# Seven-product blocks accumulated through three PSUM banks, and gram matrices on half columns, in a four-layer convolution/attention network

## The chip, the cores and the metric

The kernel runs on one core of a Trainium2 chip. A core has a matrix engine (TensorE, PE in the profile; its weight loads are listed apart as PEld), a vector engine (DVE), a scalar engine (ACT), a general engine (POOL) and a sync engine (SP) that issues transfers. Matrix products are written to PSUM, which here is eight banks of 128 partitions by 512 float32; DVE and ACT read PSUM, POOL does not in this kernel. All other tiles are in SBUF.

The metric is the device time of one execution in microseconds. The kernel before takes 1887.52 us, the median of three runs (1886.85 to 1887.64).

## What is computed

Eight images of 512 channels and 32 x 32 = 1024 positions, float32, go through four layers:

```python
# layer 0: f, g, h are 1x1 convolutions to 64 channels; batch norm and relu on f and g
z = einsum('bcn,bcm->bnm', f_x, g_x)
attn = z / svd(z)[:, 0]                       # divided by its largest singular value
z2 = einsum('bnm,bcm->bcn', attn, h_x)
x = conv1x1(z2, Wv, bv) + x
# layer 1: group norm, then attention over 1024 positions with 512 channels
h = group_norm(x); q, k, v = wq @ h, wk @ h, wv @ h
attn = softmax(q.T @ k * 512 ** -0.5); x = x + wp @ (v @ attn.T)
# layer 2: attention with 128 channels, then a projection and batch norm
t, p, g = split(W_w @ x); s = softmax(t.T @ p * 128 ** -0.5); x = x + bn(Z_w @ (g @ s.T))
# layer 3: products of signs, batch norm, residual, a PReLU
x = prelu(bn(sign(W) * mean|W| @ sign(x + bias)) + x)
```

## The kernel before

The program is traced in Python and unrolled whole. A planner in the framework orders the instructions of every engine by its own estimates of cost and inserts all waits between engines; the order of one engine in the trace is therefore not the order of the source, except for PE inside `with tc.manual_schedule(...)` (L1564), where it is written out by hand.

**The early part** (up to about 186 us). L1341 loads the eight images and forms f, g and h of each with 64-column products (`products`, L1351: two halves of an image on the two halves of the array's columns, out to partitions 0 to 63 and 64 to 127 of one bank). PSUM is split into 2 `wide` tiles of two banks and 4 single banks (L160). Images are handled in pairs j, two to a tile, 64 channels each. For each pair three gram matrices are made by `gram(j, i, lt, rhs)` (L1444): f with f (i = 0), g with g (i = 1), h with g (i = 2), each a sum over NT = 8 blocks of 128 positions. The largest singular value follows from powers of products of the first two: `first_chain(jl)` (L1128) for the pair that is used first, on full 128 x 128 matrices with zeros outside the two diagonal blocks; `chain(j)` (L1024) for the other three pairs, with its second operand as a 128 x 64 tile, its steps (`behind`) spread over the first batches.

The chain is a row of short dependent steps, so other work is set between its steps. `filler()` (L1534) is a generator of such pieces, called `todo`: two of transposes (`natural`), 16 of the weight product into `wu` (each one 128x128 by 128x512 product), the third gram of pair jl, a scaling (`scale_z`), the transposes and grams of the other pairs (`grams`, L1471, with sums of weights and biases beside them), and 16 pieces of the product into `wo`. `gram` yields twice, once after half of its blocks and once at its end, so that a gram is two pieces. Five pieces are taken before the first grams (L1555), 33 between the chain's 22 steps (L1568), and the last 25 in the first batch's entry (L1573).

The entry, `entering(0)` (L873), applies layer 0 to the first image and normalizes it: `weights0` (L293), four visits of `enter` (L409; each two products of 64 rows, L419, with a DVE addition L428 and statistics L431 for each), two tiny products for group means (L440, L447), then scale and shift (`rsqrt_eps`, L230), after which `normal` (L459) writes h, in pieces of 128x512 for the first batch, and the batches begin with `make_u` (L480). The other entries run inside the batch before.

**The batches** (eight times about 205 us). PSUM is eight single banks. Four products of each batch are written as a block scheme with seven block products in place of eight: `make_u` (2 of them), `scores1` (4), `make_v` (2) and the first part of `project2` (1), in all 9 a batch and 72 in the kernel. Each is a call of `seven` (L340). In it, `term(ps, ka, kb, first, last)` multiplies block ka of one operand with block kb of the other (2 products of 128x512, or 4 of 128x256 in `make_v`; two PE instructions for each) into a new bank if ps is None, or adds them onto what bank ps holds. In the order of the source, I number the terms 1 to 7:

1. A11 B11 into bank a; ACT copies it to c21 (L357)
2. S2 T2 into bank b; DVE adds c21 (L360)
3. S3 T3 into bank d; DVE adds c21, to c22 (L363)
4. S1 T1 into bank c; ACT copies it to c12 (L366), POOL adds c12 to c22 (L367)
5. A12 B21 onto bank a; ACT moves it to c11, or its exp (L371, L373)
6. S4 B22 onto bank c; DVE adds c21, to c12 (L376)
7. A22 T4 onto bank d; DVE adds c21 (L379)

The moves and sums are recorded at L346, L348 (`move`) and L352, L354 (`plus`), and all products at L395. So four banks are used, and three of them take a second product: bank a after three other terms, bank d after three, bank c after one (term 5). A product onto a bank waits for the read of it.

Between the terms stand other pieces: in `scores1` the last part of the batch before (`leave`) and the next batch's entry, of which each visit puts four additions and four statistics on DVE; in `make_u` almost everything of layer 2. `values1` (L547) follows `make_v`, with products in groups of four (L564).

Of the kernel before, what the change touches and what calls it, by code (L numbers as in the profile page):

```python
# [11 lines left out]
AF = mybir.ActivationFunctionType  # L12
ALU = mybir.AluOpType
# [3 lines left out]
P = 128  # L17
# [4 lines left out]
NT = N // P  # L22
# [3 lines left out]
MID = 64  # L26
# [59 lines left out]
def kernel(  # L86
# [17 lines left out]
    nc = tc.nc  # L104
    mm = nc.tensor.matmul
# [11 lines left out]
    def wide():  # L117
        return psum["wide"].tile([P, N], F32, tag="wide", name="wide")
# [4 lines left out]
    def bank():  # L123
        return psum["bank"].tile([P, HF], F32, tag="bank", name="bank")
# [17 lines left out]
    def half(i):  # L142
        return bass.ts(i, HF)

    def side(i):

        return slice(i * MID, (i + 1) * MID)
# [24 lines left out]
    def block_ones(size, value, name):  # L172

        n = P // size
        member = const.tile([P, n], F32, tag=name + "_m", name=name + "_m")
        nc.vector.tensor_reduce(
            member, ident.rearrange("p (g j) -> p g j", j=size), AX.X, ALU.add
        )
        t = const.tile([P, n, size], F32, tag=name, name=name)
        nc.vector.tensor_scalar(  # L180
            t, member.unsqueeze(2).to_broadcast([P, n, size]), value, None, ALU.mult
        )
        return t.rearrange("p g j -> p (g j)")

    mask2 = block_ones(MID, 1.0, "mask2")
# [44 lines left out]
    def rsqrt_eps(pool, var, n, name):  # L230
# [17 lines left out]
    gm = [keep.tile([P, P], F32, tag=f"gm{j}", name=f"gm{j}") for j in range(NPAIR)]  # L248
    gs_, gh_ = (
        [keep.tile([P, MID], F32, tag=f"{n}{j}", name=f"{n}{j}") for j in range(NPAIR)]  # L250
        for n in ("gg", "gh")
    )
    gg_full = keep.tile([P, P], F32, tag="gg_full", name="gg_full")
    sw3 = wpool.tile([P, CC, C // 2], F16, tag="sw3", name="sw3")
    round3 = const.tile([P, 1], F32, tag="round3", name="round3")
    nc.gpsimd.memset(round3, ROUND)
# [83 lines left out]
    def seven(term, c11, c12, c21, c22, b1=None, b2=None, exp=None, then=None):  # L340

        def move(dst, ps, bias):
            if bias is None:
                nc.scalar.copy(dst, ps)  # L346
            else:
                nc.scalar.activation(dst, ps, AF.Identity, bias=bias)  # L348

        def plus(ps, bias, u, dst):  # L350
            if bias is None:
                nc.vector.tensor_tensor(dst, ps, u, ALU.add)  # L352
            else:
                nc.vector.scalar_tensor_tensor(dst, ps, bias, u, ALU.add, ALU.add)  # L354

        pa, va = term(None, "A11", "B11", True, False)
        nc.scalar.copy(c21, va)  # L357
        yield
        _, vb = term(None, "S2", "T2", True, True)
        plus(vb, None, c21, c21)  # L360
        yield
        pd, vd = term(None, "S3", "T3", True, False)
        plus(vd, None, c21, c22)  # L363
        yield
        pc, vc = term(None, "S1", "T1", True, False)
        move(c12, vc, b2)  # L366
        nc.gpsimd.tensor_tensor(c22, c22, c12, ALU.add)  # L367
        yield
        term(pa, "A12", "B21", False, True)
        if exp is None:  # L370
            move(c11, va, b1)  # L371
        else:
            nc.scalar.activation(c11, va, AF.Exp, scale=exp)  # L373
        yield
        term(pc, "S4", "B22", False, True)
        plus(vc, b1, c21, c12)  # L376
        yield
        term(pd, "A22", "T4", False, True)
        plus(vd, b2, c21, c21)  # L379
        if then is not None:  # L380
            then()
        yield

    def product_of(lt, rhs, view=None, parts=1):

        def term(ps, ka, kb, first, last):
            fresh = ps is None
            if fresh:  # L390
                ps = bank()
            w = HF // parts
            for q in range(parts):
                for k in range(2):
                    mm(  # L395
                        out=ps[:, q * w : (q + 1) * w],
                        lhsT=lt(ka, kb, q, k),
                        rhs=rhs(ka, kb, q, k),
                        start=first and q == 0 and k == 0,
                        stop=last and k == 1,  # L400
                        skip_group_check=True,
                    )
            return ps, ps if view is None else view(ps)

        return term
# [117 lines left out]
    def scores1(env, hb, ua, es):  # L523

        scale = float(C) ** -0.5
        esum = env["small"].tile([P, N], F32, tag="esum", name="esum", bufs=1)
        for i in range(NTH):
            lo, hi = (env["e"].tile([P, N], F32, tag="e", name="e") for _ in range(2))
            es[i], es[NTH + i] = lo, hi
            term = product_of(  # L530
                lambda a, b, q, k: hb[b][:, k, bass.ts(i, P)],
                lambda a, b, q, k: ua[a][:, k, :],
            )

            yield from seven(
                term, lo[:, half(0)], hi[:, half(0)], lo[:, half(1)], hi[:, half(1)], exp=scale
            )
            nc.scalar.activation(lo[:, half(1)], lo[:, half(1)], AF.Exp, scale=scale)
            nc.scalar.activation(hi, hi, AF.Exp, scale=scale)
            if i == 0:  # L540
                nc.vector.tensor_tensor(esum, lo, hi, ALU.add)
            else:
                nc.vector.tensor_tensor(esum, esum, lo, ALU.add)
                nc.vector.tensor_tensor(esum, esum, hi, ALU.add)
        es.append(esum)
# [327 lines left out]
    def entering(n):  # L873

        b = order[n]
        f = load_f(b)

        def steps():
            while b // 2 not in ready:
                next(behind)  # L880
            if b % 2 == 0:
                for i in (b, b + 1):
                    pvs[i] = weights0(i)
            yield
            yield from enter(resident[b], f, pvs.pop(b), 2 if n else CC)

        return steps()
# [554 lines left out]


    def gram(j, i, lt, rhs):  # L1444
        ps = wide()
        for t in range(NT):
            mm(  # L1447
                out=ps[:, 0:P],
                lhsT=lt[:, t, :],
                rhs=rhs[:, t, :],  # L1450
                start=t == 0,
                stop=t == NT - 1,
            )
            if t == NT // 2 - 1:
                yield
        if i == 0 or (i == 1 and j == jl):
            nc.vector.tensor_tensor((gm[j], gg_full)[i], ps[:, 0:P], mask2, ALU.mult)
        else:
            for k in range(2):
                nc.vector.tensor_copy((gs_, gh_)[i - 1][j][side(k), :], ps[side(k), side(k)])  # L1460
        yield

    def turned_pair(j):
# [13 lines left out]
    def relu(b, i):  # L1477
        t = (fs, gs)[i][b]
        nc.scalar.activation(t, t, AF.Relu, bias=bi0[:, i : i + 1], scale=sc0[:, i : i + 1])
        if i == 0:  # L1480
            nc.sync.dma_start(out=f_dram[b], in_=t)
# [10 lines left out]
    ps = bank()  # L1492
# [5 lines left out]
    ps = bank()  # L1498
# [35 lines left out]
    def filler():  # L1534

        yield from natural("v", "k")
        load_w("p", w_p, [P, CC, C], a1, tag="v")
        yield from product(nat["q"], nat["k"], wu, True)  # L1540
        yield from gram(jl, 2, ht_pair[jl], gtl)
        scale_z()
        yield
        between = biases()
        sums = sums_u()
        for j in rest:
            for _ in grams(j):
                next(sums, None)
                yield
                if next(between, None):  # L1550
                    yield
        yield from product(nat["v"], sbw["p"], wo, False)

    todo = filler()
# [3 lines left out]
        pass  # L1558
    for i, t in ((0, ftl), (1, gtl)):
        for _ in gram(jl, i, t, t):  # L1560
            pass

    relus = iter([(2 * j + k, i) for j in rest for i in range(2) for k in range(2)])
    with tc.manual_schedule(engines={mybir.EngineType.PE}):  # L1564
        steps = entering(0)
        for k, _ in enumerate(first_chain(jl)):

            for _ in range(4 if k == 3 * NSTEP + 3 else 2 if k % 3 == 1 or k == 0 else 1):  # L1568
                next(todo, None)
            for args in (next(relus, None),):  # L1570
                if args:
                    relu(*args)
        for n in (2, 3, 3, 3, 4, 4, 6):  # L1573
            next(steps)
            for _ in range(n):
                next(todo, None)
        for _ in todo:
            pass
# [195 lines left out]
```

## Time and profile before

The profiled execution took 1886.64 us; its span, from the first to the last instruction, is 1884.9 us.

| engine | busy us | share of the span | instructions |
|---|---|---|---|
| PE | 1864.5 | 99% | 6052 |
| PEld | 962.1 | 51% | 6052 |
| DVE | 1169.7 | 62% | 2156 |
| ACT | 504.2 | 27% | 811 |
| POOL | 221.7 | 12% | 176 |

| stretch, us | what runs | length | PE busy |
|---|---|---|---|
| 0 to 108 | loads, f, g, h, weights | 108.0 | 102.57 |
| 1840 to 1885 | the last image's end | 45.0 | 34.20 |

PE's share of the chain that ended last, by line: L395 (the block products) 46%, L564 20%, L813 6%, L966 5%, L1353 5%, L1447 (grams) 1%.

How to read it: a group's line gives its source line, engine, operation, output and inputs, shape, count, then busy time (overlaps counted once), mean ns of one instruction, and the idle time of the engine before them with what ended it. In the timeline the first figure is the start in us and the second the duration of the merged instructions. A float32 product is two PE instructions, each with a weight load; they are pipelined, so that one of 512 columns lasts about 595 ns while the next starts some 430 ns after it. "issue" is time in which nothing in the profile was waited for.

### The profile page before, as it was taken

To read this page: it belongs to the slowest core of one execution; us is meant where nothing else is said; L and a number is where in the kernel's file an instruction comes from. 1 tells how busy PE (TensorE), PEld (TensorE's weight loads), DVE (VectorE), ACT (ScalarE), POOL (GpSimd) and SP (SyncE) were. 2 spreads that over 40 slices of the span, in tenths; PEclk is the share of its full clock that TensorE was granted. 3 is DMA by queue.
4 is the path that set the end of the run, shared out by engine and by line. 5 is a ranking of instruction groups with operands and counts; after the bars stand their busy time and mean duration, and the time that the engine had idled before them with its cause. 6 is when DMAs were issued, how large, how long until landed. Compare 5 with 4: busy or idle time off the path is not lost.

```text
span 1884.9 us, 16488 instructions
## 1 busy us (share of the span) xinstructions
PE 1864.5 (99%) x6052; PEld 962.1 (51%) x6052; DVE 1169.7 (62%) x2156; ACT 504.2 (27%) x811; POOL 221.7 (12%) x176
## 2 busy tenths in 40 slices
PE   8999999999999999999999999999999999999997
PEld 4366455544645455544645455544645464544653
DVE  3256776567764777567764776457743775466547
ACT  2142121144202521244202522143202521233013
POOL 0000111200120011200120011200120012101121
PEclk9999999999999999999999999999999999999999
DMA  8420000002000200002000200001000200000001
GB/s 323 162 79 6 1 15 4 1 27 76 17 0 1 88 26 4 1 27 76 16 0 1 89 25 5 1 34 67 12 0 12 89 12 0 1 34 23 12 0 47
DMA packets 25206, 66.53 MB, mean 35 GB/s; under 512 B 3553, under 2 KB 4765, under 8 KB 24477
## 3 DMA queue, kind: packets, MB, share of 16 engines
q1 hardware_dynamic: 24188, 64.96, 9.4%
q8 instruction: 50, 0.82, 0.2%
q10 hardware_dynamic: 864, 0.43, 0.1%
q14 instruction: 40, 0.32, 0.1%
q0 software_dynamic: 64, 0.00, 0.0%
HBM read 46.44 MB, written 18.94 MB: 35 GB/s over the span
## 4 chain that ended last, share of the span: by engine, by line
PE 97%; DVE 2%; ACT 1%; DMA 0%; issue 0%; POOL 0%; ACTq 0%; DVEq 0%
PE bank L395 46%; PE bank L564 20%; PE bank L813 6%; PE bank L966 5%; PE bank L1353 5%; PE bank L665 3%; PE bank L682 3%; PE bank L419 2%; PE bank L705 1%; PE wide L1393 1%; PE wide L1447 1%; PE bank L1034 1%; PE quad L1247 0%; PE bank L836 0%; PE bank L1140 0%
## 5 line engine op out<-in xcount | busy, mean ns | idle before, releaser
L564 PE MATMUL bank<-e,vt 128*128 128x512 f32 x768 | 336.2, 594 | 0.0
L564 PEld LDWEIGHTS bank<-e,vt 128*128 128x128 f32 x768 | 144.3, 190 | 172.3 <-issue 169.6
L395 PE MATMUL bank<-ut,h 128*128 128x512 f32 x384 | 182.5, 597 | 0.0
L352 DVE TENSOR_TENSOR e<-bank,e 128x512 f32<-128x512 f32 x128 | 87.6, 685 | 80.2 <-PE bank L395 79.1
L395 PE MATMUL bank<-us,hs 128*128 128x512 f32 x256 | 121.2, 596 | 0.1
L395 PEld LDWEIGHTS bank<-ut,h 128*128 128x128 f32 x384 | 71.3, 190 | 94.7 <-issue 85.3
L813 PE MATMUL bank<-tpg 128*128 128x512 f32 x256 | 115.4, 595 | 0.0
L966 PE MATMUL bank<-e,tpg 128*128 128x512 f32 x256 | 114.7, 595 | 0.0
L820 ACT ACTIVATE e<-bank 128x512 f32<-128x512 f32 x128 | 76.3, 597 | 127.6 <-PE bank L813 127.6
L395 PE MATMUL bank<-wo,h 128*128 128x256 f32 x384 | 92.8, 384 | 0.0
L367 POOL TENSOR_TENSOR e<-e 128x512 f32<-128x512 f32 x32 | 44.2, 1380 | 404.2 <-DVE both L756 101.5
L395 PE MATMUL bank<-h,wu 128*128 128x512 f32 x192 | 90.8, 595 | 0.7 <-ACT ut L357 0.7
L825 DVE TENSOR_TENSOR esum<-esum,e 128x1024 f32<-128x1024 f32 x48 | 58.8, 1225 | 34.2 <-ACT e L820 33.9
L966 PEld LDWEIGHTS bank<-e,tpg 128*128 128x128 f32 x256 | 48.1, 190 | 60.4 <-issue 60.3
L395 PEld LDWEIGHTS bank<-us,hs 128*128 128x128 f32 x256 | 47.9, 190 | 58.0 <-issue 53.6
L395 PEld LDWEIGHTS bank<-wo,h 128*128 128x128 f32 x384 | 71.0, 190 | 12.3 <-issue 3.8
L813 PEld LDWEIGHTS bank<-tpg 128*128 128x128 f32 x256 | 47.6, 190 | 55.0 <-issue 53.8
L352 DVE TENSOR_TENSOR vt<-bank,vt 128x512 f32<-128x512 f32 x64 | 44.0, 688 | 50.4 <-PE bank L395 50.1
L367 POOL TENSOR_TENSOR ut<-ut 128x512 f32<-128x512 f32 x16 | 21.8, 1366 | 448.4 <-ACT ut L348 362.9
L693 ACT ACTIVATE sg<-xt,rb 128x512 f16<-128x512 f32 x64 | 45.3, 718 | 101.4 <-DVE xt L684 97.7
L1353 PE MATMUL bank<-xt,fg 128*64 128x512 f32 x256 | 58.8, 607 | 4.7 <-DMA fg<-in_w_fg 4.7
L665 PEld LDWEIGHTS bank<-tpg,xt 128*128 128x128 f32 x512 | 59.5, 192 | 7.2 <-issue 7.2
(371 smaller groups left out, 2986.5 us busy)
## 6 DMA issues: line engine op xcount, KB each, us to landing
xt<-in_x SPq DMA_DIRECT2D x55, 512.0 KB
out<-both SPq DMA_DIRECT2D x63, 256.0 KB
rfull<-r_dram SPq DMA_DIRECT2D x15, 512.0 KB
f_dram<-f SPq DMA_DIRECT2D x8, 256.0 KB
fb<-f_dram SPq DMA_DIRECT2D x8, 256.0 KB
w<-in_w SPq DMA_DIRECT2D x1, 1024.0 KB
q<-in_w_q SPq DMA_DIRECT2D x1, 1024.0 KB
k<-in_w_k SPq DMA_DIRECT2D x1, 1024.0 KB
```

Source lines behind the costliest of these rows:

```text
L352: nc.vector.tensor_tensor(dst, ps, u, ALU.add)
L367: nc.gpsimd.tensor_tensor(c22, c22, c12, ALU.add)
L395: mm(out=ps[:, q * w : (q + 1) * w], lhsT=lt(ka, kb, q, k), rhs=rhs(ka, kb, q, k), start=first and q == 0 and k == 0, stop=last and k == 1 ...
L564: mm(out=ps, lhsT=a[:, t, bass.ts(r_, P)], rhs=e[t], start=first and t == 0, stop=last and t == NTH - 1, skip_group_check=True,)
L665: mm(out=ps[:, i, :], lhsT=xt[:, cc, bass.ts(4 * h + i, P)], rhs=sbw["tpg"][:, cc, 2 * P : 3 * P], start=cc == 0, stop=cc == CC - 1,)
L682: mm(out=ps, lhsT=sbw["z"][:, bass.ts(oc, P)], rhs=att, start=True, stop=True)
L693: nc.scalar.activation(sg[:, cc, :], xt[:, cc, half(h)], AF.Sign, bias=rb3[:, cc : cc + 1])
L813: mm(out=ps, lhsT=pt[:, 0, bass.ts(t, P)], rhs=tt[:, 0, half(h)], start=True, stop=True,)
L820: nc.scalar.activation(e[:, half(h)], ps, AF.Exp, scale=float(P) ** -0.5)
L825: nc.vector.tensor_tensor(esum, esum, e, ALU.add)
L966: mm(out=banks[h], lhsT=gt[:, t, :], rhs=es[t][:, half(h)], start=t == 0, stop=t == NT - 1,)
L1353: mm(out=banks[i][side(h), :], lhsT=w0[i][:, cc, :], rhs=xt[:, cc, half(h)], start=cc == 0, stop=cc == CC - 1,)
```

## The change

- `gm` and `gg_full` are set to zero at the start.
- `seven` uses three banks. The terms in their new order: 1 A11 B11 into bank a, ACT copies it to c11; 2 S1 T1 into bank c, ACT copies it to c22; 3 S2 T2 onto bank a, ACT copies it to c12; 4 S4 B22 onto bank c, DVE adds c12; 5 S3 T3 onto bank a, DVE adds c22; 6 A12 B21 into a new bank, DVE adds c11; 7 A22 T4 onto bank a, ACT moves it, or its exp, to c21. So bank a takes four terms and is read after each of them, with one other term between. POOL has no part in it any more; DVE has three evictions where it had four, ACT four where it had three.
- In `scores1` the exp of the other blocks follows in the other order, over hi and then the first half of lo.
- `gram` writes to a single bank. Each block of 128 positions is two products of 64 x 64, one for each image, each on its half of the array's columns and of the partitions. The copies take only what is needed, partly on ACT. It yields once.
- One piece of `todo` follows each of the first two grams; after them the pieces in the entry are 13 in place of 25.

```diff
     gg_full = keep.tile([P, P], F32, tag="gg_full", name="gg_full")
+    for g in gm + [gg_full]:
+        nc.gpsimd.memset(g, 0.0)
...
         pa, va = term(None, "A11", "B11", True, False)
-        nc.scalar.copy(c21, va)
-        yield
-        _, vb = term(None, "S2", "T2", True, True)
-        plus(vb, None, c21, c21)
-        yield
-        pd, vd = term(None, "S3", "T3", True, False)
-        plus(vd, None, c21, c22)
+        move(c11, va, None)
         yield
         pc, vc = term(None, "S1", "T1", True, False)
-        move(c12, vc, b2)
-        nc.gpsimd.tensor_tensor(c22, c22, c12, ALU.add)
+        move(c22, vc, None)
         yield
-        term(pa, "A12", "B21", False, True)
-        if exp is None:
-            move(c11, va, b1)
-        else:
-            nc.scalar.activation(c11, va, AF.Exp, scale=exp)
+        term(pa, "S2", "T2", False, False)
+        move(c12, va, None)
         yield
         term(pc, "S4", "B22", False, True)
-        plus(vc, b1, c21, c12)
+        plus(vc, b1, c12, c12)
         yield
-        term(pd, "A22", "T4", False, True)
-        plus(vd, b2, c21, c21)
+        term(pa, "S3", "T3", False, False)
+        plus(va, b2, c22, c22)
+        yield
+        _, vb = term(None, "A12", "B21", True, True)
+        plus(vb, b1, c11, c11)
+        yield
+        term(pa, "A22", "T4", False, True)
+        if exp is None:
+            move(c21, va, b2)
+        else:
+            nc.scalar.activation(c21, va, AF.Exp, scale=exp)
...
-            nc.scalar.activation(lo[:, half(1)], lo[:, half(1)], AF.Exp, scale=scale)
             nc.scalar.activation(hi, hi, AF.Exp, scale=scale)
+            nc.scalar.activation(lo[:, half(0)], lo[:, half(0)], AF.Exp, scale=scale)
...
     def gram(j, i, lt, rhs):
-        ps = wide()
+        ps = bank()
         for t in range(NT):
-            mm(
-                out=ps[:, 0:P],
-                lhsT=lt[:, t, :],
-                rhs=rhs[:, t, :],
-                start=t == 0,
-                stop=t == NT - 1,
-            )
-            if t == NT // 2 - 1:
-                yield
+            for k in range(2):
+                mm(
+                    out=ps[side(k), 0:MID],
+                    lhsT=lt[:, t, side(k)],
+                    rhs=rhs[:, t, side(k)],
+                    start=t == 0,
+                    stop=t == NT - 1,
+                )
         if i == 0 or (i == 1 and j == jl):
-            nc.vector.tensor_tensor((gm[j], gg_full)[i], ps[:, 0:P], mask2, ALU.mult)
+            g = (gm[j], gg_full)[i]
+            nc.vector.tensor_copy(g[side(0), side(0)], ps[side(0), 0:MID])
+            nc.scalar.copy(g[side(1), side(1)], ps[side(1), 0:MID])
         else:
-            for k in range(2):
-                nc.vector.tensor_copy((gs_, gh_)[i - 1][j][side(k), :], ps[side(k), side(k)])
+            nc.vector.tensor_copy((gs_, gh_)[i - 1][j], ps[:, 0:MID])
         yield
...
     for i, t in ((0, ftl), (1, gtl)):
         for _ in gram(jl, i, t, t):
-            pass
+            next(todo)
...
-        for n in (2, 3, 3, 3, 4, 4, 6):
+        for n in (2, 1, 1, 1, 2, 2, 4):
```

## The prediction

> **What bounds the kernel now.** I read the page first, then the engines by stretch, the groups by shape, PE's waits, and the timeline of three stretches.
>
> ```profile
> span 1884.9 us, 16488 instructions
> PE   8999999999999999999999999999999999999997
> DVE  3256776567764777567764776457743775466547
> PE 97%; DVE 2%; ACT 1%; DMA 0%; issue 0%; POOL 0%; ACTq 0%; DVEq 0%
> ```
> ```profile
> 108.00:186.00 78.00, 76.15 (x451) 54.69 (x452) 47.98 (x156) 24.32 (x48) 1.57 (x2) 1.00 0.10 33
> 186.00:1840.00 1654.00, 1651.60 (x5014) 848.75 (x5013) 1054.57 (x1866) 440.49 (x702) 207.18 (x146) 1.00 0.06 23
> ```
>
> The second fence's columns are the stretch, its length, busy time of PE, PEld, DVE, ACT, POOL, then PEclk. PE is busy throughout at a granted clock of 1.00. In the eight batches (186 to 1840 us) it is idle 2.4 of 1654 us. So freeing DVE or POOL there buys nothing; a new wait of PE there is paid in full, and only PE work taken away is a gain. The first chain with the first entry (108 to 186) is PE-bound as well, though with only 1.85 us idle.
>
> **Grams.** A gram before is 16 PE instructions (8 products of two passes each) at full width.
>
> ```profile
> 154.88 1.95 PE L1447 MATMUL wide<-gt 128*128 128x128 f32 x16
> 156.67 1.06 PE L1447 MATMUL wide<-gt,ht 128*128 128x128 f32 x8
> L1353 PE MATMUL bank<-xt,fg 128*64 128x512 f32 x256 | 58.8, 607 | 4.7 <-DMA fg<-in_w_fg 4.7
> L564 PE MATMUL bank<-e,vt 128*128 128x512 f32 x768 | 336.2, 594 | 0.0
> 275.83 0.64 PE L836 MATMUL bank<-esum,ones 128*32 128x256 f32 x8
> 276.40 1.99 PE L395 MATMUL bank<-wo,h 128*128 128x256 f32 x8
> 262.79 0.33 PE L1034 MATMUL bank<-cur,gm 128*128 128x64 f32 x2
> ```
>
> Before: 156.67 - 154.88 = 1.79 us, 0.112 an instruction. After: 32 instructions, 16 on each half of the columns, 64 columns wide. Two halves do run side by side: half-width L1353 takes 58.8/256 = 0.23 us an instruction where the full-width L564 takes 336.2/768 = 0.44. A 64-column pass is nearest to L1034: its two last 0.33 with 0.275 for the second, so the second starts 0.055 after the first. Lower bound 16 x 0.055 = 0.9 us. Upper bound: loads one behind another; LDWEIGHTS is 190 ns for 128 columns (L395) and 140 for 64 (L1353), 0.05 per 64 columns, 32 of them 1.7 us. Leaving the full width and coming back costs too: the L836 row holds the array 276.40 - 275.83 = 0.57 us for 2 x 0.216 = 0.43 of work, and starts 0.09 late; 0.2 in all. So a gram is 1.1 to 1.9 us; I take 1.15, since the halves of L1353 are seen side by side and their loads lie under the passes. Twelve grams: 12 x (1.15 - 1.79) = **-7.7 us of PE work**, all of it between 108 and 171 us. Copies: for i = 0 DVE's masked 128x128 (0.29) becomes a DVE and an ACT copy of 64x64 (DVE L1460 0.22); the others lose one of two copies. ACT has relus of 0.8 queued there, so its copy can start 0.8 late; the filler step now behind each gram (0.86) covers it, and without that cover it delays the chain once or twice by 0.5. The five memsets lie in POOL's first 108 us, of which 5.1 are busy, and the first is needed at 110: nothing.
>
> **The entry.** I follow the change along the rows.
>
> ```profile
> 113.36 0.49 PE L1140 MATMUL bank<-gg_full,gm 128*128 128x128 f32 x2 [0.38 <-DVE gg_full L1457]
> 153.66 0.38 PE L1168 MATMUL bank<-td,mask 128*128 128x2 f32 x2
> 160.68 1.13 PE L419 MATMUL bank<-fb,pv 64*128 64x512 f32 x4
> 176.94 0.30 PE L440 MATMUL bank<-mv,gmat 128*128 128x4 f32 x2
> 180.62 0.28 PE L447 MATMUL bank<-dev,gmat 128*128 128x4 f32 x2
> 188.55 1.98 PE L395 MATMUL bank<-h,wu 128*128 128x512 f32 x4 [0.68 <-ACT ut L357]
> ```
>
> Chain's start: grams 0 and 1 took 108.45 to 113.36 with waits; now 2 x (1.15 + 0.86, a product step) + 0.1 = 4.1: 112.55. From there to the td row run 29 filler steps. Before: 13 product (0.86), 9 half grams (0.9), 4 turns, 2 bias, 1 scale (0.9 each) = 25.6 of the 40.3 us. After: 11 product, 9 whole grams, 6 turns, 2 bias, 1 scale = 27.9. So td at 155.2. Weights0 needs 3.0 us of DVE and ACT after td (the last, DVE L1217, ends 156.67 before) and has a gram and three product steps, 3.7, before it: 159.15. First L419: 1.06 + 2 x 0.86 later, 161.95. Here the fillers fall from 25 to 13 and the cover is gone: PE has 8.6 us up to L440, DVE needs 4 visits x 3.1 (173.51 to 176.61 for the last), beginning 1.15 after L419: visits end at 175.4 and L440 comes at 175.75; PE idles some 5 us. Then two steps: L447 at 177.65. From L447 to the first two pieces of h takes 4.15 (before: pieces of 0.48 from 183.73): first product of the batches at 181.8 instead of 186.0. Its second product, A12B21, has a bank of its own now, so the 0.68 behind ACT L357 goes; T1 is ready 8.0 after L447, 185.65, two terms end at 185.25, so 0.4 is waited there. Sum: **-4.5 us** of the 7.7. Bounds: with 1.9 us a gram (all twelve lie ahead of this point) 9 more, +4.5; with no limit by DVE -7.7 and the waits of 0.47, 0.38 and 0.68, -9. No DMA moves in its queue: SP's f load and the r_dram and x loads keep their place among the steps.
>
> **The sevens.** 72 of them. Each keeps its 14 products; it gives up one DVE eviction (0.69) and one POOL sum (1.3) and gains an ACT eviction (0.59): DVE -50, POOL -95, ACT +42 us, nothing of it on the path. New are three ACT links (term 3 waits for term 1's eviction, 4 for 2's, 5 for 3's) and a DVE link (7 for 5's), each with one term between; before, only 4 to 6 was as short.
>
> ```profile
> 255.82 1.98 PE L395 MATMUL bank<-ut,h 128*128 128x512 f32 x4
> 257.64 1.88 PE L395 MATMUL bank<-us,hs 128*128 128x512 f32 x4
> 259.36 1.88 PE L395 MATMUL bank<-ut,h 128*128 128x512 f32 x4
> 257.84 0.59 ACT L357 COPY e<-bank 128x512 f32<-128x512 f32 x1 [2.48 <-PE bank L395]
> 262.43 0.67 DVE L352 TENSOR_TENSOR e<-bank,e 128x512 f32<-128x512 f32 x1
> ```
>
> A term starts 1.72 after the one before and ends 1.88 after its own start, so a link has 1.56 us. An eviction starts 0.04 after its term (257.80 to 257.84) and PE restarts 0.05 after it (ACT L357 ended 188.50 before the 188.55 row): ACT 0.68, DVE 0.8 are needed. Spare: 0.9 and 0.75. In the trace ACT starts terms 1, 4 and 5 within 0.3 except in the second scores seven (1.03, and 0.8 in the first): 8 x 0.12. DVE starts term 6, the nearest to the new term 5, 0.1 to 0.6 late, 0.92 in the first scores seven of seven batches: 7 x 0.12. Together 1.8; DVE has two evictions less ahead of it there (1.4 us), so I take **+1.5**, bounds 0 and 30 (below). Behind a waiting term stands all of PE; the next eviction on ACT or DVE comes as much later, and they have room. Exp of scores1: the same three pieces in another order, under ACT's 27%.
>
> **Sum.** 1884.9 - 4.5 + 1.5 = 1881.9 span; the profiled run took 1886.64, 1.7 more than its span, and the median is 0.9 above that run: **1884.5 us**, own range 1881 to 1888.
>
> **Rivals.**
> (1) Entry not bound by DVE: the planner lets its visits start earlier or PE's fillers spread, the whole -9 comes. For: PE is the bound before. Against: 12 fewer fillers over a DVE run of 12.4 us. 1880.
> (2) Weight loads of the halves follow one another: gram 1.9 us, L395 at +4.5, links 1.5: 1893.5. For: the full-width gram is spaced like its loads (0.112). It turns from gain to loss at a gram of 1.4, where 12 x 0.25 has used up the 3 us.
> (3) DVE is late where the DVE link is. In the third and fourth scores seven DVE is held by the entry's visits and starts term 2 at 262.43, 2.9 after 259.52, in seven batches. If the planner puts that burst on term 5, PE waits 2.9 + 0.8 - 1.56 = 2.1, 14 times 29 us; it decides from a lateness of 0.75. Between a quarter and all of it: 1891 to 1913, half of it 1899. For: DVE is 77% busy there. Against: by term 6 the burst is over (0.1).
> (4) The change doesn't do what it says: the planner moves terms apart (A12B21 is free to move) and the links cost nothing, but PE's queue was the limit of the grams, not their width, and nothing is gained: 1887.5. For: 0.112 an instruction is also what 128x1 products take (L1427, eight in 0.92). Against: L1034's 0.055.
> (5) Loads don't hide at all. If a load waits for every pass on the same rows, a gram is 32 x (0.055 + 0.05) = 3.4, 12 x 1.6 = +19: 1906. The row speaks against it: L564's passes are 0.44 apart with a load of 0.19 between each two. The Trainium skill, "TensorE: Matmul & The Clock Gate", section "The mechanism", states that a load overlaps running products only where the row group differs, and both halves of a gram use all rows; by that rule this rival would be the forecast, and the trace disagrees.
>
> **Chances.** Forecast 0.42, (1) 0.16, (2) 0.17, (3) 0.15, (4) 0.06, (5) 0.04. A change under 0.2% (3.8 us) can't be told from none: faster is under 1883.7, slower over 1891.3. The border cuts the forecast's range: 0.19 of it is faster, 0.23 same. With (1) faster 0.34, with (4) and some of (2) same 0.35, slower 0.31. Range 1879.5 to 1896: it leaves out (5), the upper part of (3) and little below.
>
> **What would show it.** Gram rows of 16 pairs lasting 1.1 to 1.3 us (over 1.8: rival 2). L440 near 175.7 behind DVE's last bn_aggr, with PE idle some 5 us before it; the first L395 near 182. In 186 to 1840 PE's idle time up from 2.4 to about 4, its waits naming ACT L348 or DVE L354 before a chained term; over 10 is rival 3. Wrong is the forecast if the stretch of the batches changes in length by more than 4 us, or if the first L395 isn't earlier.

## The result, and the profile after

The changed kernel takes 1883.57 us (median of 20 runs), the kernel before 1887.24 us beside it (20 runs): 3.67 us less, a ratio of 0.998 with a 95% interval of 0.9974 to 0.9987. One of the 20 runs was disturbed (2168.59 us); the other nineteen lie between 1882.94 and 1884.04. The prediction was 1884.5, and the change is smaller than the 3.8 us that I set as the border to "no change", though the interval excludes a ratio of 1.

Lines of the page after, the ones shown of before: the span, the busy tenths of PE and of DVE in 40 slices, and the chain that ended last by engine.

```profile
span 1881.5 us, 16558 instructions
PE   8998999999999999999999999999999999999997
DVE  3256776467764676567764676357643666355447
PE 96%; DVE 2%; ACT 1%; issue 0%; DMA 0%; POOL 0%; DVEq 0%; ACTq 0%
```

PE is still what bounds it, but its fourth slice (141 to 188 us) has fallen from 9 to 8: a hole has come at the end of the early part. The engines by stretch, columns as in the prediction (stretch, length, busy time of PE, PEld, DVE, ACT, POOL, granted clock):

```profile
108.00:186.00 78.00, 71.17 (x646) 45.48 (x644) 47.07 (x153) 27.06 (x55) 1.57 (x2) 0.98 0.10 33
186.00:1840.00 1654.00, 1652.46 (x5017) 849.75 (x5018) 1006.39 (x1792) 481.54 (x776) 106.58 (x74) 1.00 0.06 23
```

From 108 to 186 PE is idle 78.00 - 71.17 = 6.8 us where it was idle 1.85, and the clock is 0.98 for 1.00. In the batches it is idle 1.5 us where it was idle 2.4; DVE and POOL have been relieved as forecast (1054.57 to 1006.39 and 207.18 to 106.58), ACT loaded (440.49 to 481.54), to no effect on PE. PE's timeline in the early part (start, duration, then the idle time and its releaser in brackets):

```profile
112.94 0.49 PE L1141 MATMUL bank<-gg_full,gm 128*128 128x128 f32 x2 [1.02 <-ACT gg_full L1460]
...
142.66 1.15 PE L1450 MATMUL bank<-ft 128*64 128x64 f32 x32
143.74 0.49 PE L1141 MATMUL bank<-both 128*128 128x128 f32 x2
...
155.90 0.38 PE L1169 MATMUL bank<-td,mask 128*128 128x2 f32 x2
...
163.04 1.13 PE L420 MATMUL bank<-fb,pv 64*128 64x512 f32 x4
...
170.45 1.98 PE L1394 MATMUL wide<-p,nat_v 128*128 128x512 f32 x4
175.28 0.59 PE L441 MATMUL bank<-mv,gmat 128*128 128x4 f32 x2 [2.85 <-DVE mv L440]
175.73 3.39 PE L1394 MATMUL wide<-p,nat_v 128*128 128x512 f32 x4
178.96 0.28 PE L448 MATMUL bank<-dev,gmat 128*128 128x4 f32 x2
...
182.76 1.96 PE L396 MATMUL bank<-h,wu 128*128 128x512 f32 x4
187.00 1.98 PE L396 MATMUL bank<-hs,su 128*128 128x512 f32 x4 [2.28 <-DVE hs L336]
```

A gram holds PE for 143.74 - 142.66 = 1.08 us; it was 1.79. Two new waits end the early part, 2.85 us at L441 and 2.28 us at the first block product that needs T1 (`hs`). Between them stands a row to compare with the one at 170.45: the same four passes of L1394 take 3.39 us in place of 1.98. PE's windows around the hole (columns as above) show why:

```profile
173.00:175.20 2.20, 0.00 (x0) 0.00 (x0) 2.13 (x5) 0.00 (x0) 0.00 (x0) 1.00 0.00 0
175.20:180.00 4.80, 4.72 (x10) 2.50 (x11) 0.87 (x7) 0.00 (x0) 0.48 (x1) 0.64 0.00 0
```

In the hole DVE is busy and PE does nothing; in the 4.8 us after it PE is busy at a granted clock of 0.64 in the mean. Those four passes alone lose 3.39 - 1.98 = 1.4 us.

The two traces set side by side, by the start of `values1` (L565) in each batch: after is ahead by 2.52 us in the first batch, 3.23 in the second, 3.19 to 3.34 up to the seventh, 3.41 in the eighth; and 3.42 at the end of the span. So 2.5 us come from the early part with the beginning of the first batch, and 0.9 from the rest. PE's waits from 186 to 1840 us (total, times, longest), first of the kernel before, then of the one after:

```profile
PE bank L1034 <- DVE gm L1046: 1.1, 1, 1.1
PE bank L395 <- ACT ut L357: 0.7, 1, 0.7
PE bank L682 <- DVE att L975: 0.5, 1, 0.5
```
```profile
PE bank L396 <- DVE hs L336: 2.3, 1, 2.3
PE bank L1035 <- DVE gm L1047: 0.5, 1, 0.5
```

Only 1.0 us of the 2.28 us lies behind 186 us. No wait on a chained bank is listed in 72 sevens.

### The profile page after: what moved, and what is told of

The parts are those of the page before. It is cut to its first block, busy times and chain, and to the rows that moved or that the text cites. A ratio compares the mean times of both kernels' runs of the same rounds, so it can differ in the third digit from the quotient of the medians.

```text
span 1881.5 us, 16558 instructions
## 1 busy us (share of the span) xinstructions
PE 1857.0 (99%) x6244; PEld 952.1 (51%) x6244; DVE 1118.1 (59%) x2077; ACT 545.7 (29%) x888; POOL 121.8 (6%) x109
## 4 chain that ended last, share of the span: by engine, by line
PE 96%; DVE 2%; ACT 1%; issue 0%; DMA 0%; POOL 0%; DVEq 0%; ACTq 0%
PE bank L396 46%; PE bank L565 21%; PE bank L967 6%; PE bank L814 6%; PE bank L1354 5%; PE bank L666 3%; PE bank L683 3%; PE bank L420 1%; PE bank L706 1%; PE wide L1394 1%; PE bank L1450 1%; PE bank L1035 1%; PE bank L837 0%; PE quad L1248 0%; PE bank L1141 0%
## 5 line engine op out<-in xcount | busy, mean ns | idle before, releaser
L565 PE MATMUL bank<-e,vt 128*128 128x512 f32 x768 | 336.2, 594 | 0.0
L565 PEld LDWEIGHTS bank<-e,vt 128*128 128x128 f32 x768 | 144.3, 190 | 172.3 <-issue 167.9
L396 PE MATMUL bank<-ut,h 128*128 128x512 f32 x384 | 178.3, 597 | 0.0
L396 PE MATMUL bank<-us,hs 128*128 128x512 f32 x256 | 115.3, 592 | 0.0
L354 DVE TENSOR_TENSOR e<-bank,e 128x512 f32<-128x512 f32 x96 | 66.1, 689 | 63.2 <-PE bank L396 44.7
L348 ACT COPY e<-bank 128x512 f32<-128x512 f32 x96 | 56.1, 584 | 115.0 <-PE bank L396 114.6
L236 POOL TENSOR_TENSOR r_r<-r_v,minus_half 128x4 f32<-128x4 f32 (+1 forms) x11 | 10.9, 988 | 1073.4 <-DVE r_v L235 1067.9
L354 DVE TENSOR_TENSOR vt<-bank,vt 128x512 f32<-128x512 f32 x48 | 33.2, 691 | 67.3 <-PE bank L396 66.6
L348 ACT COPY vt<-bank 128x512 f32<-128x512 f32 x64 | 37.3, 583 | 122.3 <-PE bank L396 122.3
L348 ACT COPY ut<-bank 128x512 f32<-128x512 f32 x48 | 28.1, 585 | 123.4 <-PE bank L396 123.4
```

Of the source, the lines that this page charges most:

```text
L396: mm(out=ps[:, q * w : (q + 1) * w], lhsT=lt(ka, kb, q, k), rhs=rhs(ka, kb, q, k), start=first and q == 0 and k == 0, stop=last and k == 1 ...
L565: mm(out=ps, lhsT=a[:, t, bass.ts(r_, P)], rhs=e[t], start=first and t == 0, stop=last and t == NTH - 1, skip_group_check=True,)
```

## The experiments

The theory at the start of the experiments: the narrow grams give some 8 us, of which the hole at the end of the entry, its slow clock and the wait for T1 give back about 5; the new sevens cost nothing. Rivals: the grams' gain was never on the path; the sevens cost what was forecast. A "shift" below is the start of `values1` against the profiled run of before. The first product waits for the first load, and so the start of each run's PE work differs (4.73 us before, 4.89 after, 4.09 to 4.55 in the experiments), so that shifts are good to about half a microsecond.

**Grams and entry alone.** The sevens of before, all the rest of the change. Seen from after:

```diff
-        move(c11, va, None)
+        nc.scalar.copy(c21, va)
...
+        nc.gpsimd.tensor_tensor(c22, c22, c12, ALU.add)
...
+            nc.scalar.activation(lo[:, half(1)], lo[:, half(1)], AF.Exp, scale=scale)
             nc.scalar.activation(hi, hi, AF.Exp, scale=scale)
-            nc.scalar.activation(lo[:, half(0)], lo[:, half(0)], AF.Exp, scale=scale)
```

> The changed kernel with the four-bank sevens (and scores1's order of exp) of before: only the grams, the memsets and the fillers stay changed. Theory (the gain of 3.4 us of span is 2.5 before the batches and 0.9 in them): PE idle 2.8 us ahead of the first tiny mean product, first block product near 182.8, and 0.9 us of the gain given back: 1884.5. Rival (the sevens make the gain, the early part only shifts work): 1886 or more. Rival (the links cost something that the early gain hides): 1882.5 or less.

Measured: 1886.28 us, beside 1887.23 of before (ratio 0.9996, 0.9987 to 1.0005), a miss by 1.8, and the first rival's number. The narrow grams with their entry alone gain 0.95 us, which the interval can't tell from nothing. PE's waits there:

```profile
PE bank L442 <- DVE mv L441: 2.8, 1, 2.8
PE bank L1036 <- DVE gm L1048: 1.1, 1, 1.1
...
PE bank L397 <- ACT ut L359: 0.7, 1, 0.7
...
PE bank L397 <- DVE hs L337: 0.7, 1, 0.7
PE bank L684 <- DVE att L977: 0.5, 1, 0.5
```

The hole is there, and the waits of the old sevens with it. But the trace of this kernel is ahead by 1.63 us in the first batch and 1.51 in the eighth, and by 0.32 at the end of the span: 1.2 us are lost in the last image's end. About 1.0 of it is a single DVE instruction, first in the kernel before, then here:

```profile
1872.64 0.55 DVE L732 TENSOR_SCALAR up<-both,nc,ps 128x512 f32<-128x512 f32 x1
```
```profile
1871.23 1.54 DVE L734 TENSOR_SCALAR up<-both,nc,ps 128x512 f32<-128x512 f32 x1
```

POOL's next sum starts 0.01 us ahead of it here, and 0.10 behind it in before; that this makes it slow is not shown. So the 0.95 us understate what the entry and the grams gain ahead of the batches.

**The new sevens alone.** Kernel before with the new `seven` and the order of the exp, full-width grams and 25 fillers.

```diff
-        for n in (2, 1, 1, 1, 2, 2, 4):
+        for n in (2, 3, 3, 3, 4, 4, 6):
```

> The kernel before with the three-bank sevens alone. Theory: the links have 0.75 us and more of spare, PE waits nowhere for them, and DVE's relief takes some waits away: 1886.4, 0.9 under before, and no wait of PE on a block product's eviction in the batches over 0.3 us. Rival (each link costs a little, as forecast): 1888.5 to 1889. Rival (nothing at all from the sevens): 1887.3.

Measured: 1885.21 us (ratio 0.999, 0.9981 to 0.9999), 2.0 below before. What the forecast put down as a cost of 1.5 is a gain, 1.2 more than expected before the run; 0.6 of it may be this run's earlier start. It shifts by 1.42 in the first batch and 1.61 to 1.83 afterwards; no chained bank is waited for. The two parts alone give 0.95 + 2.0 = 2.9, and by the trace 1.2 more without the loss at the end of the first; both together give 3.67.

**The grams at full width.** After, with one product of 128 x 128 for each block of positions again; bank, copies' engines, yields and fillers stay.

```diff
-            for k in range(2):
-                mm(
-                    out=ps[side(k), 0:MID],
-                    lhsT=lt[:, t, side(k)],
-                    rhs=rhs[:, t, side(k)],
...
+            mm(
+                out=ps[:, 0:P],
+                lhsT=lt[:, t, :],
+                rhs=rhs[:, t, :],
```

> The changed kernel with full-width products in the grams (8 of 128x128 in the single bank, copies from the diagonal blocks), all else as changed. Theory (all twelve grams lie on the path to the entry, whose end DVE sets): 12 x (1.79 - 1.08) = 8.5 us later, first block product at 191, 1892. Rival (the entry's idle PE would absorb the width, the gain came from the fillers): 1884 to 1886.

Measured: 1891.06 us (ratio 1.0021, 1.0012 to 1.003), 7.5 above after. 12 x 0.71 = 8.5 us of PE work, and 7.5 of it is on the path: the grams' gain is real and nearly all of it is paid out, which ends the rival that it was hidden. And it follows that the rest of the entry's edit, which this kernel shares, costs: with old grams and new fillers it is slower than before, in spite of the sevens' 2.0.

**Is it the clock?** After, with three products that nobody reads set in the hole, so that PE is not idle there.

```diff
-        for n in (2, 1, 1, 1, 2, 2, 4):
+        for k, n in enumerate((2, 1, 1, 1, 2, 2, 4)):
...
+            if k == 4:
+                spare = bank()
+                for i in range(3):
+                    mm(out=spare, lhsT=nat["q"][:, i, 0:P], rhs=nat["k"][:, i, :], start=i == 0, stop=i == 2)
```

> The changed kernel with three more products of 128x512, whose result is not used, after the last visit's fillers, where PE stands idle for 2.8 us. Theory (the idle PE lowers the granted clock to 0.64 in the 4.8 us after it, so that four passes take 3.39 us in place of 1.96): the clock stays at 1.00, the mean product comes at the same 175.3, the deviation product 1.6 us earlier at 177.3, first block product near 181.2: 1882, faster with 2.6 us more of PE work. Rival (the slow passes come from a transfer or a code load at that time, or the clock drops anyway): 1883.6 or later, with the passes still over 3 us.

Measured: 1883.81 us (ratio 0.9982, 0.9973 to 0.9992): no gain, a miss. The timeline and the windows of this kernel show that the clock was cured in one place and lost in the next:

```profile
175.21 1.96 PE L1394 MATMUL wide<-p,nat_v 128*128 128x512 f32 x4
...
180.82 1.95 PE L396 MATMUL bank<-h,wu 128*128 128x512 f32 x4
185.05 3.40 PE L396 MATMUL bank<-hs,su 128*128 128x512 f32 x4 [2.28 <-DVE hs L336]
```
```profile
175.00:180.00 5.00, 5.00 (x15) 2.61 (x16) 2.01 (x14) 0.00 (x0) 1.02 (x1) 1.00 0.00 0
185.00:190.00 5.00, 4.95 (x11) 2.59 (x12) 3.90 (x7) 0.59 (x1) 0.55 (x1) 0.66 0.00 0
```

With the hole filled, the four passes take 1.96 us again and the first block product starts 1.94 earlier (180.82 for 182.76). Then PE waits 2.28 us for T1 as before, and this time that wait is followed by a mean clock of 0.66 (1.00 in after at this place): the four passes behind it take 3.40 us (1.98 in after, at 187.00). The slow clock is thus shown to be the cost of the 3.39 row, and it follows a wait, not a place in the program. Both waits have to go.

**The hole covered by work that is due anyway.** One filler fewer at the chain's end, and the entry's 13 become 14 in another order, with five where the hole was.

```diff
-            for _ in range(4 if k == 3 * NSTEP + 3 else 2 if k % 3 == 1 or k == 0 else 1):
+            for _ in range(3 if k == 3 * NSTEP + 3 else 2 if k % 3 == 1 or k == 0 else 1):
...
-        for n in (2, 1, 1, 1, 2, 2, 4):
+        for n in (1, 1, 1, 1, 5, 1, 4):
```

> The changed kernel with the pieces of filler spread otherwise: 3 in place of 4 behind the chain's end, and 1, 1, 1, 1, 5, 1, 4 in the entry in place of 2, 1, 1, 1, 2, 2, 4; no work added or taken away. Theory (a chain of latencies sets the entry, pieces ahead of it delay it and are missing in its gaps): visits start 1.7 us earlier, first mean product 173.5, deviation product 174.6, first block product 178.8; the wait for the first difference stays (2.3 us) and now draws the drop of the clock on itself, as in the run with three spare products (1.6 us): gain over the changed kernel 2.5 to 3, 1881. Rival (PE's work alone sets the end of the entry): 1883.6.

Measured: 1881.33 us (ratio 0.9969, 0.9957 to 0.9981), 2.2 below after, as expected. L441 starts at 173.63 with 0.27 idle, the first block product at 178.76; the 2.28 us for T1 remain, and the window of 180 to 185 us has a mean clock of 0.79.

**The order that the prediction had assumed.** A12 B21 as the second term, in the very first seven alone; once with the covered hole and once without.

```diff
+        if early:
+            _, vb = term(None, "A12", "B21", True, True)
+            plus(vb, b1, c11, c11)
+            yield
...
+                early=not i and len(resident) == 2,
```

> The kernel with the fillers spread otherwise, and besides, in the first block product's first seven alone, A12 B21 (its own bank, needs no difference) as second term. Theory (two gaps, either of which drops the clock; here both are closed): no idle of PE over 0.6 us between 108 and 200, clock 1.00 throughout, gain over the changed kernel 5 to 6 us: 1878. Rival (what is won in the entry is lost to the first batch's chain and sums): 1881.

> The changed kernel with A12 B21 as second term in the first seven alone, fillers as changed. Theory: the 2.3 us wait falls to 0.6 or less, the clock's drop at the first gap stays: gain 1.7 us over the changed kernel: 1881.9. Rival (as with the spare products, the gain is lost within 10 us): 1883.6.

Measured: with cover 1877.68 us (ratio 0.9951, 0.9938 to 0.9965), without 1882.09 (0.9974, 0.9964 to 0.9984). The timeline and the windows with cover:

```profile
173.10 0.38 PE L446 MATMUL bank<-mv,gmat 128*128 128x4 f32 x2 [0.28 <-DVE mv L445]
...
178.24 3.67 PE L401 MATMUL bank<-h,wu 128*128 128x512 f32 x8
...
182.47 3.84 PE L401 MATMUL bank<-hs,su 128*128 128x512 f32 x8 [0.23 <-DVE hs L336]
```
```profile
175.00:180.00 5.00, 5.00 (x12) 2.01 (x11) 3.73 (x14) 1.01 (x1) 1.02 (x1) 1.00 0.00 0
180.00:185.00 5.00, 4.77 (x15) 2.28 (x14) 5.00 (x7) 1.09 (x2) 0.00 (x0) 1.00 0.00 0
```

Both waits are down to 0.28 and 0.23 and the clock stays at 1.00. In after they cost (2.85 - 0.28) + (3.39 - 1.96) + (2.28 - 0.23) = 6.05 us, and the times differ by 5.9. The order alone gives 1.5 (1883.57 to 1882.09), with the hole covered 3.65 (1881.33 to 1877.68): where the wait for T1 also slows the clock, taking it away pays twice. This is the fastest version, 9.4 us below before.

**Does the covered entry need the new sevens?** The fillers of the covered kernel and the narrow grams, with the sevens of before.

> The kernel with the fillers spread otherwise and the changed grams, but with the four-bank sevens of before in all batches (A12 B21 comes second in the first one by the planner's own choice). Theory (with the entry covered, the sevens' share is what they give in the batches, 0.9 to 1.2, and the 0.7 behind ACT's copy at the first one): 1877.7 + 1.8 = 1879.5. Rival (their share is the whole 2.0 and more of the run with the sevens alone): 1880.5 or more. Rival (nothing): 1877.7.

Measured: 1882.6 us (ratio 0.9973, 0.9963 to 0.9984), 4.9 above the best version; the rival's side of the expectation. Its shift is 5.23 in the first batch and 4.67 in the eighth, the best version's 8.41 and 9.28: 3.2 us of the difference arise up to `values1` of the first batch, 1.4 later. In the last image's end of its profiled execution it loses another 1.05 us, as the kernel with grams and entry alone does and with the same slow DVE instruction (1.55 us), which is no part of what the sevens give. PE's waits say where most of the rest is:

```profile
PE bank L1036 <- DVE gm L1048: 1.1, 1, 1.1
...
PE bank L684 <- DVE att L977: 0.9, 1, 0.9
PE bank L397 <- DVE hs L337: 0.9, 1, 0.9
...
PE bank L397 <- ACT ut L359: 0.7, 1, 0.7
```

In the best version the one for `ut` is gone, those for `att` and `hs` are 0.2 each, and `gm` is waited for 0.8 in two parts. Against the covered kernel with the changed order of terms but without the early A12 B21 (1881.33) it is only 1.3, though that one waits 2.28 us for T1 with a drop of the clock behind it, and this one 0.9 without.

**The best version with full-width grams.**

> The kernel with the fillers spread otherwise and A12 B21 second in the first seven, with full-width products in the grams. Theory (ten grams lie in the chain and two ahead of it, all on the path): 12 x 0.71 = 8.5 more than with half columns: 1886. Rival (half of it only, since the chain's own latency would hide narrow grams): 1882.

Measured: 1885.54 us (ratio 0.999, 0.9981 to 0.9999), 7.9 above the best version. The width of the grams is worth the same with the waits gone as with them (7.5), so the hole is no part of its price.

**How much room the links have.** After, with one more read of bank a by DVE between terms 5 and 7 (it repeats a value that term 7's move overwrites), then with two.

```diff
         plus(va, b2, c22, c22)
+        nc.vector.tensor_copy(c21, va)
```

> The changed kernel with one more DVE read of bank a after term 5 of every seven (a copy of 128x512 to c21, which term 7 overwrites): 72 more DVE instructions, the bank held 0.65 us longer. Theory (the DVE link has 0.75 us of spare): 1883.6 to 1885. Rival (the link is already at its limit, and each 0.65 is paid): 72 x 0.65 = 47, 1930.

> The changed kernel with two more DVE reads of bank a after term 5 of every seven (144 copies of 128x512 to c21, which term 7 overwrites). Theory (a link has 1.56 us, the three reads take 0.04 + 2.0 + 0.05 = 2.1): PE waits 0.5 us at most sevens for term 7, with DVE named, 72 x 0.5 = 36 over the changed kernel less where other work stands between: 1905 to 1925. Rival (the planner moves other terms in front and hides it, as DVE's sum of work is still under PE's): under 1895.

Measured: one read 1886.28 us (ratio 0.9996, 0.9987 to 1.0005), 2.7 above after and 1.3 over the range expected; two 1904.66 (1.0091, 1.0076 to 1.0107), 21 above. The copy lasts 0.69 us (128x512). With one, PE waits before term 7 in four of 72 sevens, 1.9 us in all; DVE and PE of this kernel at 712 us:

```profile
713.86 0.85 DVE L1048 STREAM_TRANSPOSE gm<-cur 32x32 f32<-32x32 f32 x4
714.73 0.69 DVE L371 COPY vt<-bank 128x512 f32<-128x512 f32 x1
715.43 1.29 DVE L354 TENSOR_TENSOR vt<-bank,vt 128x512 f32<-128x512 f32 x2
716.18 1.99 PE L397 MATMUL bank<-wo,hs 128*128 128x256 f32 x8 [0.43 <-DVE vt L354]
```

There the transposes of the next pair's chain run on DVE first, and the two reads of the bank behind them end late. Everywhere else 0.69 more fits: the spare that I had put at 0.75 for DVE's link is about right.

The 1904.66 of two reads lies 0.3 under the range expected, but the trace doesn't bear out what that range was made from, 0.3 us in each seven. PE's waits on chained banks stay under 0.8 us in total. The planner has moved other products in between terms 5 and 7, among them the two passes of one 64-row product of the next entry, away from the other products that it stood beside. PE's timeline, first after, then with two reads:

```profile
251.16 1.99 PE L420 MATMUL bank<-fb,pv 64*128 64x512 f32 x8
253.08 1.98 PE L396 MATMUL bank<-ut,h 128*128 128x512 f32 x4
```
```profile
250.47 1.12 PE L422 MATMUL bank<-fb,pv 64*128 64x512 f32 x2
251.52 1.98 PE L398 MATMUL bank<-ut,hs 128*128 128x512 f32 x4
253.44 1.98 PE L422 MATMUL bank<-fb,pv 64*128 64x512 f32 x6
255.35 1.98 PE L398 MATMUL bank<-ut,h 128*128 128x512 f32 x4
```

Eight passes of 64 rows hold PE for 253.08 - 251.16 = 1.92 us. Two and six hold it for 1.05 + 1.91 = 2.96: here passes on two halves of the rows run side by side only where they stand together. Added up from start to start, these 128 passes take 45.7 us in place of 31.1: 14.6 of the 21 us. Another 4.0 are spread over the 1,568 block passes of 512 columns, and 1.3 are passes of L1394 at a slow clock that lasts longer here (last section). So a late link is paid in the order of PE's queue before it is paid in waits, and the price of a waiting link by itself remains open.

## Why the prediction came out near, point by point

The sum said 3.0 us less in the span, and 3.4 was measured. That it came so near is luck: the early part gave 2.5 us for 4.5, the batches gave 0.9 where 1.5 had been put down as a cost, and the two errors cancel.

- **Grams: right.** 1.15 us taken, 1.08 measured, 12 x 0.71 = 8.5 us of PE work for 7.7. The loads of the two halves lie under the passes. (The upper bound's 1.7 should read 32 x 0.05 = 1.6.) Rival (2), 1.9 us, and rival (5), 3.4 us, fall by this row. For (5) the Trainium skill ("TensorE: Matmul & The Clock Gate", section "The mechanism") has a load overlap only passes on another row group, and in the same section also lets a load into a background weight buffer go ahead of running passes. The trace disagrees with the first here too, with 32 loads and passes on all rows in 1.08 us; whether the second is the reason no trace shows.
- **Copies: the delay seen, its cover not there.** "ACT has relus of 0.8 queued there" is what happened, once: the copy of `gg_full` stood behind a relu and PE waited 1.02 us. The sum had counted on "the filler step now behind each gram (0.86) covers it"; but the last product steps on PE stand ahead of the first gram and inside it (106.26 and 108.78), and none behind the second. Without cover I had written 0.5 once or twice. The chain started at 112.94 (112.55 forecast), the td row came at 155.90 (155.2), L420 at 163.04 (161.95).
- **The hole: right in place, with its cost missed.** L441 was forecast at 175.75 behind DVE and came at 175.28 behind DVE. The hole is 2.85 us, not 5: L420 started 1.1 later, PE's work behind it took 9.4 us and not 8.6 (163.04 to 172.43), and L441 came 0.5 earlier. But "Then two steps: L447 at 177.65" is wrong: it came at 178.96, as PE returned to a slow clock and the steps took 1.4 us longer. With PE kept busy the row is 1.96 us.
- **The failed step of the early sum: "A12B21, has a bank of its own now, so the 0.68 behind ACT L357 goes; T1 is ready 8.0 after L447, 185.65, two terms end at 185.25, so 0.4 is waited there".** That T1 would be late was right. That the planner would use the free bank to bring A12 B21 forward was assumed: it kept S1 T1 second, and PE waited 2.28 us. Written out by hand the order saves 1.5 us, and 3.65 with the clock undisturbed. With the hole's late end this makes -2.5 of the -4.5.
- **The failed step of the batches: "I take +1.5".** It is -0.9, and PE's idle time in the batches went from 2.4 to 1.5 us, not to about 4. The links cost nothing at all: no wait on a chained bank, and the spare, tried with one read more, is about the 0.75 worked out. What failed is the addition of single late evictions as if each were paid; a lateness below the spare costs nothing. And a gain was not looked for: the waits of before at `gm` (1.1) and `att` (0.5) shrink to 0.5 and nothing, as does the one at ACT L357. The new sevens alone give 2.0 us.
- **Rivals.** (1), the whole early gain, did not come by itself, but it was there to be had: with the hole covered and the order mended 1877.68, against the 1880 worked out. (3) fell: no product waits behind DVE's burst. (4) fell with the full-width grams, 7.5 us slower, though its half on the links, that they cost nothing, held.

## What to carry to other kernels

Where a stretch is bound by one engine, taking its work away pays only as long as the engines beside it can follow: look for the next late result, and lay work that is due anyway in front of it rather than at the end. A bank that becomes free is no order; if a sum rests on a product coming earlier, write that order down. And look in the trace for what an experiment really did: a time that agrees with the expectation can have come about in another way, as with the two reads.

## What was not expected of the hardware

- **PE's clock falls for a fixed step after a short wait.** The 0.64, 0.66 and 0.79 above are means. Split where the clock changes, the windows of after are (columns as in the prediction):

```profile
171.79:175.20 3.41, 0.64 (x2) 0.00 (x0) 3.34 (x8) 0.00 (x0) 0.00 (x0) 1.00 0.21 68
175.20:178.62 3.42, 3.34 (x6) 1.79 (x7) 0.71 (x6) 0.00 (x0) 0.00 (x0) 0.50 0.00 0
182.03:185.44 3.41, 2.69 (x6) 0.68 (x4) 3.40 (x9) 1.60 (x2) 0.00 (x0) 1.00 0.00 0
185.44:188.86 3.42, 1.86 (x5) 0.90 (x6) 3.39 (x4) 0.00 (x0) 0.00 (x0) 1.00 0.00 0
```

  The clock is at 0.50 for 3.41 us, and so it is with the three spare products (185.48 to 188.89) and in the covered kernel (182.95 to 186.36). After's second wait, 2.28 us from 184.72 on, falls on the border of two such steps, with PE busy 2.69 and 1.86 us of them, and the clock stays. Such steps can be laid end to end over all 13 traces, from the first rise of the clock to the last image's end. Of those at a clock of 1.00, the eight in which PE was busy 0.58 to 1.45 us are each followed by a step at 0.50 (with two reads more, by two), and none of the others, in which it was busy 1.77 us or more, is. So where a wait falls among the steps decides, and a drop costs at most half a step, 1.7 us. This is read from one execution of each kernel; no run was made to test it. The Trainium skill ("TensorE: Matmul & The Clock Gate", section "What's actually happening") has the array drop to half its clock after an idle window of about 3.4 us, in windows that don't start with the kernel. The trace agrees on the half, on the length and that the place of a wait counts; that PE must be idle for 3.4 us is not borne out, as a wait of 2.28 was enough.
- **Products on two halves of the rows shared the array only in neighbouring places of the queue**: eight passes took 1.92 us together, 2.96 us when two stood apart.
- **Narrow products on two halves of the columns** start 1.08/32 = 0.034 us apart, where the full-width ones of 128 columns start 0.112 apart, with a load to each.
